# A slot table for each pass, scans in place of the decays, dt spread from SBUF, B turned once a chunk, and a second pass on 32 columns

## The chip, the cores and the metric

The kernel runs on one NeuronCore of one Trainium2 chip. The metric is the device time of one execution in microseconds (us), and the number quoted is the median over runs. Durations of instructions come from one profiled execution, which has a time of its own. The engines are called by their names in the profile: PE (matmul) and PEld (its weight load), DVE (vector), ACT (scalar), POOL and SP (which issues the DMAs).

## What is computed

The input x has shape (1, 64, 256, 128): 64 channels, T = 256 time steps, F = 128 frequencies, all in float32. Two layers follow each other.

Layer 0 runs Mamba blocks first along time and then along frequency, each in both directions. The core of one direction, with 128 inner channels and 16 states per channel, is

```
xz = in_proj(rmsnorm(u)); x, z = split(xz)
x  = silu(causal_conv4(x) + conv_b)
dt, B, C = split(x_proj(x), [4, 16, 16])
dt = softplus(dt_proj(dt) + dt_proj_b)
h[t] = exp(dt[t] * A) * h[t-1] + dt[t] * B[t] * x[t]      # per channel and state
y[t] = sum over states of h[t] * C[t]
out  = out_proj((y + x * Dp) * silu(z)) + u
```

The outputs of both directions go through one more linear map (tlin, flin) and are added to the input. Layer 1 normalises globally, runs a convolutional LSTM over 32 windows, and adds the result to its input. The change concerns layer 0 alone.

## The kernel before

**Tiling.** `Stage` is built twice: stage 0 is the pass along time, stage 1 the pass along frequency. A pass is cut into 64 chunks of 512 tokens (2 sequences of 256 steps, or 4 of 128). The inner channels lie on the 128 partitions. For the recurrence the 2048 pairs of channel and state in a direction are laid out again: the channels are cut into NB = 4 blocks of 32, and one block with 4 groups j of states fills 128 partitions. With two states g side by side this gives 8 **slots** a direction and 16 a chunk. One slot is one scan of 128 x 1024 elements.

**One slot S**, with its names and lines: `decays` (L599, ACT) makes dA = exp(A * dt) from rep, which holds dt repeated for the four state groups, into one of NRING = 4 buffers; a copy of zeros (L596) cuts the sequences apart. `inputs` (L579, PE) makes bx = dt * B * x in PSUM by 32 matmuls of dtxT (dt * x, turned) with D, a diagonal matrix that holds B; two buffers of two banks each. `recur` (L607, DVE) scans dA and bx into h, one of NH = 7 buffers. `outputs` (L613, POOL) multiplies h by C. `add_up` (L622, PE) folds the states of four slots into y in PSUM. In these matmuls the profile counts every float32 matmul as two passes.

**One chunk**: `load`, `squares`, `means` (pm), `rms`, `normalise` (unp, spread by DMA), `project_x` (px, L328 and L329), `project_z` (pz), `silus`, `step_sizes` (pv, L370), `softplus` (dt), `dt_away` (L394: dt goes to HBM four times, as the tile there), `spread_dt` (L486: rep comes back, 512 KB at a time), `project_bc` (pb, then bc, which holds B and C; C goes to HBM as away, L442), `spread_c` (L480), `times_x` (dtx, POOL), `turn` (dtx to pt and dtxT; B to bt, both by transposes on PE), and `diagonal` (L471, DVE: D = mask * bt, four times a direction). At the end of a direction `gate` multiplies y by silu(z) into yz (DVE, L638) and `skip` starts the next y as x * Dp (ACT). `close` (po) and `keep` finish the chunk.

**Order.** Every engine runs its instructions in the order in which they are emitted (a manual schedule). `run` walks through the slots; at slot S it emits the scan of S, the product of S - 1, the inputs and decays of S + 2, and then what the table HEAD names for that slot. HEAD is one list of (slot, step) for both passes; negative slots lie in the chunk before. All DMAs are issued from SP, in order too. `first` does the steps of a pass's first chunk by hand.

Of the kernel before, what the change touches and what calls it, by code (L numbers as in the profile page):

```python
# [29 lines left out]
F32 = mybir.dt.float32  # L30
# [30 lines left out]
NRING = 4  # L61
NREP = 3
RESPOND = 12
NH = 7
LAG = 2
# [7 lines left out]
HEAD = (  # L73
    (-12, "load"),
    (-7.5, "squares"),
    (-6, "means"),
    (-6, "rms"),
    (-5, "normalise"),
    (-2, "project_x", 0),
    (-1, "project_z"),  # L80
    (0, "project_x", 1),
    (6, "silus"),
    (6, "step_sizes"),
    (7, "softplus"),
    (8, "dt_away", 0),
    (8, "project_bc", 0, 1),
    (8.5, "times_x", 0),
    (9.5, "spread_dt", 0, 0),
    (10, "turn", 0),
    (10, "spread_c", 0, 0),  # L90
    (11, "diagonal", 0, 0, 0),
    (12, "spread_dt", 0, 1),
    (12.5, "times_x", 1),
    (13, "diagonal", 0, 0, 1),
    (13.5, "spread_c", 0, 1),
    (14, "dt_away", 1),
    (15, "diagonal", 0, 1, 0),
    (17, "diagonal", 0, 1, 1),
    (17, "spread_dt", 1, 0),
    (17.5, "spread_c", 1, 0),  # L100
    (18, "turn", 1),
    (19, "diagonal", 1, 0, 0),
    (20, "spread_dt", 1, 1),
    (21, "diagonal", 1, 0, 1),
    (21.5, "spread_c", 1, 1),
    (23, "diagonal", 1, 1, 0),
    (25, "diagonal", 1, 1, 1),
)
SECOND = tuple(x for x in HEAD if x[0] >= 12 and x[1] != "dt_away")


class Mamba:
# [3 lines left out]
    def __init__(self, ctx, tc, cols, room, d):  # L116
# [12 lines left out]
        for i in range(4):  # L129
            for n, t, rows, width in (  # L130
                ("g1", self.G1, P, P),
                ("g2", self.G2, P, P),
                ("wdt", self.Wdt, P, P),
                ("w2", self.W2, P, C),
            ):
                t.append(cp.tile([rows, width], F32, name=f"{n}{i}", tag=f"{n}{i}"))
        for i in range(2):
            self.Wz.append(cp.tile([P, P], F32, name=f"wz{i}", tag=f"wz{i}"))
            self.W3.append(cp.tile([P, 2, C], F32, name=f"w3{i}", tag=f"w3{i}"))
# [15 lines left out]
        self.xdt = take(RANK, 8, P).rearrange("p (i n) -> p i n", i=8)  # L155
# [13 lines left out]
    def load(self, first):  # L169
        dma, d = self.nc.sync.dma_start, self.d  # L170
        if first:
# [3 lines left out]
            dma(out=self.xdt, in_=d["dt_proj"])  # L175
# [22 lines left out]

    def dt(self, i, ps):
        self.nc.tensor.matmul(ps[:, 0:P], lhsT=self.xdt[:, i], rhs=self.xdt[:, 4 + i], start=True, stop=True)  # L200
        self.nc.vector.tensor_copy(self.Wdt[i], ps[:, 0:P])
# [23 lines left out]
class Stage:  # L225
# [8 lines left out]
    def __init__(self, ctx, m, stage, L, X, src, moments, gates):  # L234
# [5 lines left out]
        self.time = stage == 0  # L240
        n = f"s{stage}_"
        self.io = ctx.enter_context(tc.tile_pool(name=n + "io", bufs=1))
        self.wk = ctx.enter_context(tc.tile_pool(name=n + "wk", bufs=1))
        self.st = ctx.enter_context(tc.tile_pool(name=n + "st", bufs=NH))
# [5 lines left out]
        self.ps_bt = ctx.enter_context(tc.tile_pool(name=n + "bt", bufs=1, space=PSUM))  # L250
# [4 lines left out]
        self.zeros = fixed.tile([P, 2, 2, self.nseq // 2, 1], F32, name="zeros", tag="zeros")  # L255
        nc.gpsimd.memset(self.zeros, 0.0)
        self.dA = []
        for k in range(NRING):
            self.dA.append(fixed.tile([P, 2, 2, self.nseq // 2, L], F32, name=f"dA{k}", tag=f"dA{k}"))
        self.at, self.spare = {}, []  # L260

        self.y = self.ps_y.tile([P, NTOK], F32, name="y", tag="y")
# [29 lines left out]
    def means(self, ch):  # L292
        n = self.nseq // 2
        self.pm = self.mm("pm")[:, 0 : n * self.L].rearrange("p (n l) -> p n l", n=n)
# [8 lines left out]
    def normalise(self, ch):  # L303
        nc, n, L, unp = self.nc, self.nseq // 2, self.L, self.unp
        xn = self.io.tile([P, n, L], F32, name="xn", tag="xn")
        nc.gpsimd.tensor_mul(xn, self.at["u", ch], self.rs)
# [35 lines left out]
    def project_x(self, ch, d):  # L342
        i = 2 * self.stage + d
        px = self.mm("px")
        xs = self.wk.tile([P, NTOK], F32, name="xs", tag="xs", bufs=4)
# [4 lines left out]
    def project_z(self, ch):  # L350
        pz = [self.mm("pz") for _ in range(2)]
        self.gated(pz)
        for d in range(2):
            zs = self.wk.tile([P, NTOK], F32, name="zs", tag="zs", bufs=5)
# [11 lines left out]
    def step_size(self, ch, d):  # L366

        i = 2 * self.stage + d
        self.at["pv", d] = pv = self.mm("pv")
        self.nc.tensor.matmul(pv, lhsT=self.m.Wdt[i], rhs=self.at["xs", ch, d], start=True, stop=True)  # L370

    def step_sizes(self, ch):
        for d in range(2):
            self.step_size(ch, d)
# [8 lines left out]
    def softplus(self, ch):  # L383
        self.nc.scalar.preload_act_table_set(SOFTPLUS)
# [4 lines left out]
    def dt_away(self, ch, d):  # L389

        there = self.dram.tile([NJ, DB, NB, NTOK], F32, name="there", tag="there")
        for b in range(NB):
            dt = self.at["dt", ch, d][DB * b : DB * (b + 1)]
            self.nc.sync.dma_start(  # L394
                out=there[:, :, b].rearrange("j d t -> d j t"), in_=dt.unsqueeze(1).to_broadcast([DB, NJ, NTOK])
            )
        self.at["there", ch, d] = there

    def in_turns(self, ap, order):

        return ap.rearrange(order, i=2, u=NU)

    def times_x(self, ch, d):

        dtx = self.wk.tile([P, NTOK], F32, name="dtx", tag="dtx")
        natural, own = "p (i u c) -> p i u c", "p (u i c) -> p i u c"
# [7 lines left out]
    def project_bc(self, ch, *ds):  # L414
# [3 lines left out]
        for n in range(2):  # L418
# [13 lines left out]
            self.in_turns(bc[rows], "p (u i c) -> p i u c"), self.in_turns(pb[rows], "p (i u c) -> p i u c")  # L432
# [3 lines left out]
        for d in ds:  # L436
            away = self.dram.tile([NS // 2, NR, 2, 2, NTOK // 2], F32, name="away", tag="away")
            for g in range(2):
                first = 2 * NBC + NBC * d + NS // 2 * g
                c = bc[first : first + NS // 2].rearrange("p (i t) -> p i t", i=2)  # L440
                for i in range(2):
# [852 lines left out]
```

## Time and profile before

| | |
|---|---|
| median of 3 runs | 7161.71 us (7147.89 to 7171.97) |
| the profiled execution's own time | 7169.17 us |
| its span | 7167.4 us |
| first scan of pass one starts at | 45.46 us |
| last scan of pass one ends, first of pass two starts | 3211 us, 3243.5 us |
| last scan of pass two ends | 6473.5 us |
| the rest (LSTM) | 694 us |
| bytes moved by DMA | 921.86 MB, of which 310.38 MB written to HBM |

The profile's page lists the busy time of each engine and its share of the span, the groups of instructions with the idle time ahead of them and what ended it, and the DMA issues. A window gives the same busy times for a stretch; the two passes are two windows. The list of waits adds up, for each engine and line, the time for which it stood and whom it stood for. The timeline lists instructions in order of time. Overlap of one instruction's end with the next one's start makes the duration of an instruction some 80 ns longer than its share of a busy engine.

### The profile page before, as it was taken

The numbers are of one execution on the slowest core, as the hardware profiler recorded it, in microseconds if no ns is written. First come the engines' busy times: TensorE is split into PE (matmuls) and PEld (weight loads), VectorE is DVE, ScalarE is ACT, GpSimd is POOL, SyncE is SP. The second block draws the span as 40 slices with busy tenths as digits, with TensorE's granted clock in tenths as the row PEclk, the third lists the DMA queues.
The fourth block names the chain that finished last, engine by engine and source line by source line (L and its number), as shares of the span: only waits on it lengthen the run. The fifth ranks groups of instructions, "written<-read, shape, count | busy, mean of one in ns | idle before, by whom it ended". The sixth has DMA issues, their size and how long they took to land.

```text
span 7167.4 us, 327118 instructions
## 1 busy us (share of the span) xinstructions
PE 5830.0 (81%) x150024; PEld 3482.0 (49%) x150024; DVE 6368.4 (89%) x4166; ACT 4829.9 (67%) x8730; POOL 5567.1 (78%) x2898
## 2 busy tenths in 40 slices
PE   7878777777877787877888888787887878778998
PEld 4444444444444444444444444444444444447887
DVE  7999898889999999988988889999989899896887
ACT  6767676767767677767777677777767677763333
POOL 6888888778888888877887778888888788784554
PEclk9999999999999999999999899999999999999999
DMA  5555555555555555545555555555555555550000
GB/s 134 152 146 139 145 139 145 133 145 139 143 149 138 146 152 136 149 116 150 137 149 133 148 132 147 135 144 150 130 143 133 140 134 144 132 140 35 14 16 17
DMA packets 412666, 921.86 MB, mean 129 GB/s; under 512 B 52372, under 2 KB 142100, under 8 KB 411288
## 3 DMA queue, kind: packets, MB, share of 16 engines
q1 hardware_dynamic: 411288, 900.93, 48.8%
q8 instruction: 1177, 19.28, 1.1%
q14 instruction: 201, 1.65, 0.1%
HBM read 557.32 MB, written 310.38 MB: 121 GB/s over the span
## 4 chain that ended last, share of the span: by engine, by line
PE 25%; DVE 11%; ACT 8%; issue 6%; DMA 2%; POOL 2%; SPq 1%; DVEq 0%; POOLq 0%; ACTq 0%
DVE h L607 8%; PE bx L579 6%; PE cv L1048 6%; ACT dA L599 4%; PE y L622 3%; DVE D L471 2%; PE px L328 2%; PE px L329 1%; POOL h L613 1%; PE pv L370 1%; DMA unp<-xn 1%; PE pz L334 1%; PE pg L1104 1%; PE both L1160 1%; ACT L387 1%
## 5 line engine op out<-in xcount | busy, mean ns | idle before, releaser
L613 POOL TENSOR_TENSOR h<-h,C 128x1024 f32<-128x1024 f32 x2048 | 4826.7, 2374 | 974.8 <-DVE h L607 781.2
L607 DVE TENSOR_TENSOR_SCAN h<-dA,bx 128x1024 f32<-128x1024 f32 x2048 | 4618.0, 2276 | 497.4 <-PE bx L579 310.4
L579 PE MATMUL bx<-D,dtxT 64*32 64x128 f32 x131072 | 2509.0, 281 | 1180.5 <-DVE h L607 799.5
L579 PEld LDWEIGHTS bx<-D,dtxT 64*32 64x32 f32 x131072 | 1926.4, 108 | 2312.4 <-issue 1125.7
L599 ACT ACTIVATE dA<-rep,cols 128x510 f32<-128x510 f32 (+1 forms) x4096 | 2648.1, 710 | 171.2 <-DMA rep<-there 163.7
L471 DVE TENSOR_TENSOR D<-mask,bt 128x1024 f32<-128x1024 f32 x1026 | 1227.6, 1197 | 34.6 <-PE bt L458 34.0
L622 PE MATMUL y<-h,fold 128*32 128x512 f32 x8192 | 1106.4, 659 | 5.4 <-POOL h L613 5.4
L347 ACT ACTIVATE xs<-px,cols 128x512 f32<-128x512 f32 x252 | 173.4, 688 | 898.5 <-PE px L329 898.5
L622 PEld LDWEIGHTS y<-h,fold 128*32 128x32 f32 x8192 | 243.5, 117 | 612.8 <-issue 566.2
L407 POOL TENSOR_TENSOR dtx<-dt,xs 128x512 f32<-128x512 f32 x256 | 327.3, 1279 | 71.7 <-ACT dt L380 71.2
L460 ACT COPY dtxT<-pt 128x512 f32<-128x512 f32 x256 | 149.9, 585 | 300.6 <-PE pt L456 300.6
L328 PE MATMUL px<-unp,g 128*128 128x512 f32 x504 | 313.7, 706 | 46.5 <-DMA unp<-xn 46.3
L370 PE MATMUL pv<-xs,wdt 128*128 128x512 f32 x512 | 278.4, 669 | 34.0 <-ACT xs L364 31.8
L329 PE MATMUL px<-unp,g 128*128 128x512 f32 x504 | 277.3, 633 | 0.5 <-issue 0.5
L638 DVE TENSOR_TENSOR yz<-y,zs 128x512 f32<-128x512 f32 x256 | 172.7, 675 | 74.9 <-PE y L622 72.7
L355 ACT COPY zs<-pz 128x512 f32<-128x512 f32 x252 | 134.9, 586 | 154.5 <-PE pz L334 148.6
L1171 POOL TENSOR_TENSOR y<-v,X 128x512 f32<-128x512 f32 x32 | 40.6, 1269 | 231.2 <-DVE v L1169 231.2
L596 ACT COPY dA<-zeros 128x4 f32<-128x4 f32 (+1 forms) x1024 | 197.4, 193 | 5.4 <-DVE h L607 4.0
L634 ACT ACTIVATE y<-xs,cols 128x512 f32<-128x512 f32 x256 | 175.6, 686 | 9.5 <-DVE yz L638 9.5
L1120 ACT ACTIVATE a<-pg,cols,scale 128x488 f32<-128x488 f32 x128 | 86.5, 756 | 135.6 <-DVE pg L1118 135.6
L680 PE MATMUL po<-yz,w 128*64 128x256 f32 x1024 | 172.5, 400 | 0.9 <-ACT dA L599 0.9
L380 ACT ACTIVATE dt<-pv,cols 128x512 f32<-128x512 f32 x256 | 164.3, 684 | 12.7 <-issue 6.2
(190 smaller groups left out, 5195.8 us busy)
## 6 DMA issues: line engine op xcount, KB each, us to landing
there<-dt SPq DMA_DIRECT2D x1024, 256.0 KB
rep<-there SPq DMA_DIRECT2D x512, 512.0 KB
C<-away SPq DMA_DIRECT2D x512, 512.0 KB
away<-bc SPq DMA_DIRECT2D x1024, 32.0 KB
unp<-xn SPq DMA_DIRECT2D x504, 64.0 KB
u<-in_x SPq DMA_DIRECT2D x128, 64.0 KB
out<-y SPq DMA_DIRECT2D x32, 256.0 KB
w<-in_W_ih_f SPq DMA_DIRECT2D x10, 512.0 KB
```

The source lines that it names most:

```text
L328: nc.tensor.matmul(self.seqs(px), lhsT=m.G1[i], rhs=self.unp[:, :, first : first + L], start=True, stop=False)
L329: nc.tensor.matmul(self.seqs(px), lhsT=m.G2[i], rhs=self.unp[:, :, second : second + L], start=False, stop=True)
L370: self.nc.tensor.matmul(pv, lhsT=self.m.Wdt[i], rhs=self.at["xs", ch, d], start=True, stop=True)
L407: self.nc.gpsimd.tensor_mul(self.in_turns(dtx, own), self.in_turns(self.at["dt", ch, d], natural), self.in_turns(self.at["xs", ch, d], nat ...
L471: self.nc.vector.tensor_mul(D, self.m.mask.unsqueeze(1).unsqueeze(1).to_broadcast([P, n, 2, W]), b.unsqueeze(3).to_broadcast([P, n, 2, W]),)
L579: self.nc.tensor.matmul(bx[DB * j : DB * (j + 1), i, :, u], lhsT=dtxT[rows, u, DB * b : DB * (b + 1)], rhs=D[rows, u, j], start=True, stop ...
L596: nc.scalar.copy(dA[:, :, :, :, first : first + 1], self.zeros)
L599: nc.scalar.activation(dA[:, :, g, :, live], rep[:, :, :, live], AF.Exp, scale=m.A[:, k, n : n + 1])
L607: self.nc.vector.tensor_tensor_scan(h[:, step], dA[:, step], bx[:, step], 0.0, ALU.mult, ALU.add)
L613: self.nc.gpsimd.tensor_mul(h, h, self.at["C", ch, d, q])
L622: nc.tensor.matmul(y[DB * b : DB * (b + 1)].rearrange("p (i t) -> p i t", i=2), lhsT=self.m.fold, rhs=hs[b][:, g], start=False, stop=q == ...
L1048: self.nc.tensor.matmul(t[:, g, :, 0:n_out], lhsT=wts[s][:, gate * P : (gate + 1) * P], rhs=self.parts[n][:, :, s : s + n_out], start=s == ...
```

## The change

- **Tables.** HEAD becomes two tables, BY_Q for pass one and BY_HALF for pass two, with a slot for every piece of a chunk, four `spread_dt` a direction among them. `AT` gives the slots of fold, gate and close for each pass.
- **Scans write over decays.** dA and h are one tile: ACT writes the decays into h, the scan reads and overwrites it. There are 12 buffers in pass one, and 7 of double size in pass two. Decays are made four slots ahead. The zeros are written for every new tile.
- **dt from SBUF.** dt no longer goes to HBM: for each block b of 32 channels, four DMAs copy 32 rows of dt straight into the four quarters of rep.
- **dt projection.** The product of x_proj's dt rows and dt_proj is no longer formed (`dt` and `xdt` go). The dt rows ride with C in `project_bc`, and `step_size` multiplies 32 rows of bc by dt_proj, so it now follows `project_bc` and its copies.
- **B.** B of both directions is turned by four transposes of 64 rows into a fixed half bank (bt); pm, po and the LSTM's small sums use the other half of that bank (small).
- **Pass two 32-wide.** A slot there is two of the four sequences with four states, instead of four sequences with two. Chunks of 128 columns are cut into four rows of 32 instead of two of 64, so that D has 16 states by 32 columns, made in two products a direction instead of four. bx takes 32-row weights. C comes in one DMA of 1 MB a direction. The fold of a direction is done for the even slots and then for the odd ones, in 16 matmuls of 256 columns each.
- In the emitted order of pass two, the gate at slot 8k + 2 stands ahead of the odd slots' fold at the same slot: for that half of the tokens z multiplies what y holds by then, which is the skip term alone.

```diff
-NRING = 4
-NREP = 3
-RESPOND = 12
-NH = 7
-LAG = 2
+NSLOT = 12
+NPAIR = 7
+RESPOND = 13
+AHEAD = 2
+AT = ((2, 3, 3), (1, 2, 2))
-HEAD = (
...
-SECOND = tuple(x for x in HEAD if x[0] >= 12 and x[1] != "dt_away")
+BY_Q = (
+    (-11.5, "load"),
+    (-6.5, "squares"),
+    (-5.5, "means"),
+    (-5.5, "rms"),
+    (-4.5, "normalise"),
+    (-2, "project_x", 1),
+    (-1.5, "project_x", 0),
+    (0.5, "project_z"),
+    (7, "silus"),
+    (7, "project_bc", 0, 1),
+    (8, "softplus"),
+    (8.5, "c_away", 0),
+    (8.5, "c_away", 1),
+    (9, "times_x", 0),
+    (10, "spread_dt", 0, 0),
+    (10, "turn_b"),
+    (11.5, "spread_dt", 0, 1),
+    (11.5, "spread_dt", 0, 2),
+    (11.5, "turn_x", 0),
+    (12, "spread_dt", 0, 3),
+    (12.5, "diagonal", 0, 0, 0),
+    (13.5, "diagonal", 0, 0, 1),
+    (14, "diagonal", 0, 1, 0),
+    (15.5, "spread_dt", 1, 0),
+    (15.5, "diagonal", 0, 1, 1),
...
+    (19, "diagonal", 1, 0, 0),
+    (21, "diagonal", 1, 0, 1),
+    (21, "spread_c", 1, 0),
+    (24, "diagonal", 1, 1, 0),
+    (24, "spread_c", 1, 1),
+    (25, "diagonal", 1, 1, 1),
+)
+BY_HALF = (
...
+    (-7, "means"),
+    (-7, "rms"),
+    (-5.5, "normalise"),
+    (-1.5, "project_x", 0),
+    (1, "project_z"),
+    (4, "project_x", 1),
+    (6, "silus"),
+    (6, "project_bc", 0, 1),
+    (7.5, "softplus"),
+    (7.5, "spread_dt", 0, 0),
+    (7.5, "turn_b"),
+    (8, "c_away", 0),
+    (8.5, "times_x", 0),
+    (9, "diagonal", 0, 0, 0),
...
+    (11, "diagonal", 0, 0, 1),
...
+    (14, "diagonal", 1, 0, 0),
...
+    (18, "diagonal", 1, 0, 1),
+    (19, "spread_dt", 1, 2),
+    (22.5, "spread_c", 1, 0),
+)
...
     def step_size(self, ch, d):
...
-        self.nc.tensor.matmul(pv, lhsT=self.m.Wdt[i], rhs=self.at["xs", ch, d], start=True, stop=True)
+        rows = slice(2 * NBC + NBC * d, 2 * NBC + NBC * (d + 1))
+        self.nc.tensor.matmul(pv, lhsT=self.m.Wdt[self.stage][rows], rhs=self.bc[rows], start=True, stop=True)
...
+    def turn_b(self, ch, ds=(0, 1)):
+        nc = self.nc
+        rows = slice(NBC * ds[0], NBC * (ds[-1] + 1))
+        for u in range(NU):
+            nc.tensor.transpose(
+                self.bt[:, ds[0] : ds[-1] + 1, u], self.bc[rows, P * u : P * (u + 1)], self.m.ident[rows, rows]
+            )
...
-        t = self.wk.tile([P, 2, NTOK], F32, name="rep", tag="rep", bufs=NREP)
-        there = self.at["there", ch, d].rearrange("j d b t -> (j d) b t")
-        self.nc.sync.dma_start(out=t, in_=there[:, 2 * h : 2 * h + 2])
+        t = self.wk.tile([P, NTOK], F32, name="rep", tag="rep", bufs=6 if self.time else 3)
+        for j in range(NJ):
+            self.nc.sync.dma_start(
+                out=t[DB * j : DB * (j + 1)], in_=self.at["dt", ch, d][DB * b : DB * (b + 1)]
+            )
...
+    def decays(self, k):
+        nc, m, L = self.nc, self.m, self.L
+        ch, d, _, b = self.where(2 * k)
+        first, live = self.ends(d)
+        h = self.st.tile([P, 4, 4, L], F32, name="h", tag="h")
+        nc.scalar.copy(h.rearrange("p i s t -> p (i s) t")[:, :, first], self.zeros)
+        rep = self.at["rep", ch, d, b].rearrange("p (i l) -> p i l", i=4)
+        for s in range(4):
+            n = 4 * b + s
+            nc.scalar.activation(h[:, :, s, live], rep[:, :, live], AF.Exp, scale=m.A[:, 2 + d, n : n + 1])
...
     def recur(self, S):
...
-        h = self.st.tile([P, 2 * NTOK], F32, name="h", tag="h")
-        dA = self.dA[S % NRING].rearrange("p i g n l -> p (i g n l)")
-        bx = self.at.pop(("bx", S)).rearrange("p i g u c -> p (i g u c)")
-        self.nc.vector.tensor_tensor_scan(h[:, step], dA[:, step], bx[:, step], 0.0, ALU.mult, ALU.add)
+        h = self.at["h", S][:, step]
+        bx = self.at.pop(("bx", S)).rearrange("p i s u c -> p (i s u c)")[:, step]
+        self.nc.vector.tensor_tensor_scan(h, h, bx, 0.0, ALU.mult, ALU.add)
...
+    def sums(self, S):
+        n = S - self.fold_at
+        if self.time:
+            return range(n - 4, n) if n > 0 and n % 4 == 0 else ()
+        first = n // 8 * 8 - 8 + n % 8
+        return range(first, first + 8, 2) if n % 8 < 2 and n >= 8 else ()
+
+    def ahead(self, S):
+        if self.time:
+            for n in (4, 5) if S % 16 == self.pause else () if S % 16 == self.pause + 1 else (4,):
+                if 0 <= S + n < 16 * NCH:
+                    self.decay(S + n)
+        elif S % 2 == 0 and 0 <= S + 4 < 16 * NCH:
+            self.decays(S // 2 + 2)
```

## The prediction

> **What bounds the kernel now.** I read the page's busy line first, then the two Mamba passes as windows, then DVE's waits, then the groups, then the timeline.
>
> ```profile
> PE 5830.0 (81%) x150024; PEld 3482.0 (49%) x150024; DVE 6368.4 (89%) x4166; ACT 4829.9 (67%) x8730; POOL 5567.1 (78%) x2898
> ```
> ```profile
> 45.00:3211.00 3166.00, 2518.90 (x73223) 1415.77 (x73216) 2910.42 (x1660) 2258.34 (x4007) 2605.61 (x1212) 0.96 0.55 142
> 3243.00:6473.00 3230.00, 2605.98 (x73385) 1472.70 (x73378) 2910.11 (x1660) 2294.35 (x4217) 2607.91 (x1212) 0.93 0.55 139
> ```
> The columns of the windows are length, then busy time of PE, PEld, DVE, ACT, POOL, clock, DMA share, GB/s. Each window is 64 chunks of 16 slots. Per chunk, pass one takes 3166/64 = 49.5 us and pass two 50.5; DVE is busy 45.5 in both, PE 39.4 and 40.7, POOL 40.7, ACT 35.3 and 35.8. VectorE bounds both passes, with 256 and 320 us of idle time left, and PE and POOL stand only 5 us a chunk behind it.
>
> ```profile
> L613 POOL TENSOR_TENSOR h<-h,C 128x1024 f32<-128x1024 f32 x2048 | 4826.7, 2374 | 974.8 <-DVE h L607 781.2
> L607 DVE TENSOR_TENSOR_SCAN h<-dA,bx 128x1024 f32<-128x1024 f32 x2048 | 4618.0, 2276 | 497.4 <-PE bx L579 310.4
> ...
> L599 ACT ACTIVATE dA<-rep,cols 128x510 f32<-128x510 f32 (+1 forms) x4096 | 2648.1, 710 | 171.2 <-DMA rep<-there 163.7
> L471 DVE TENSOR_TENSOR D<-mask,bt 128x1024 f32<-128x1024 f32 x1026 | 1227.6, 1197 | 34.6 <-PE bt L458 34.0
> ```
> ```profile
> DVE h L607 <- PE bx L579: 310.4, 261, 4.5
> DVE h L607 <- ACT dA L599: 157.8, 96, 10.1
> DVE yz L638 <- PE y L622: 72.7, 66, 6.0
> ```
> A chunk is 16 scans, 8 products D and 2 products with z. DVE's idle time is mostly scans waiting for bx, then for decays. The timeline of DVE (columns: start, duration) gives the pitch, start to start, which is what an instruction really costs here:
>
> ```profile
> 3258.10 1.20 DVE L471 TENSOR_TENSOR D<-mask,bt 128x1024 f32<-128x1024 f32 x1
> 3259.21 4.46 DVE L607 TENSOR_TENSOR_SCAN h<-dA,bx 128x1024 f32<-128x1024 f32 x2
> ...
> 3265.18 4.46 DVE L607 TENSOR_TENSOR_SCAN h<-dA,bx 128x1024 f32<-128x1024 f32 x2
> 3269.55 1.20 DVE L471 TENSOR_TENSOR D<-mask,bt 128x1024 f32<-128x1024 f32 x1
> ```
> D takes 3259.21 - 3258.10 = 1.11 us, a scan (3269.55 - 3265.18)/2 = 2.19.
>
> [...] 2276 ns against 1197 for a product of the same size, so writing over the decays saves no scan time. [...]
>
> **The change, part by part.**
>
> *Second pass 32-wide.* D holds 16 states by 32 columns instead of twice 8 by 64: two products a direction instead of four. 64 chunks x 4 x 1.11 = 284 us off the bounding engine, 41.0 us a chunk left (45.5 - 4.4). bx keeps 32 matmuls of 128 columns a slot, now on 32 rows; as in each u eight different tiles are addressed, I take today's 1.16 us. Bounds: half of that if row tiles overlap further (no gain, it is not the bound), or twice, the second rival. The fold becomes 16 matmuls of 256 columns instead of 8 of 512: a wave of four took 0.43 us (1.86 a fold); po's 256-column waves took 0.24, so 8 x 0.24 = 1.9: +0.1 to +0.2 us a fold, beside the scans.
>
> *Slots and order in pass one.* What DVE loses now comes in slots 15, 1 and 3, where px (1.9 us), pz (1.1), px and a fold (1.86) stand between two bx; these prices are start to start in the timeline between 1500 and 1550 us, as are po and the waves below and above. PE has two bx buffers, so PE work between two bx is free only up to 2 x 2.19 - 2 x 1.2 = 2.0 us, plus 1.11 for each D on DVE meanwhile. The table puts both px (3.8 us) at slot 14, and D at 12, 13, 14 and 15. Worked from scan 14's end: bx of 16 at 0 to 1.2, px to 5.0, bx of 17 to 6.2; DVE runs D to 1.1, scan 15 to 3.3, D to 4.4, scan 16 to 6.6: no wait. pz follows bx of 18 and a fold bx of 19, each with one slot of room; pb waits for the silus at slot 7, under D at 8 and 9. With decays four slots ahead in place of two, the 158 us of waits for ACT go too. What is late next is chance, such as this stop of PE in the middle of a tile, which DVE's next scan waits out:
>
> ```profile
> 1540.87 1.12 PE L579 MATMUL bx<-D,dtxT 64*32 64x128 f32 x60
> ...
> 1544.94 0.41 PE L579 MATMUL bx<-D,dtxT 64*32 64x128 f32 x4 [2.95 <-issue]
> ...
> 1545.49 2.29 DVE L607 TENSOR_TENSOR_SCAN h<-dA,bx 128x1024 f32<-128x1024 f32 x1 [1.87 <-PE bx L579]
> ```
> PE's waits put 372 us in 266 times to "issue" before bx. I keep 1.1 us a chunk: 45.5 + 1.1 = 46.6, so 2982 us, **-184**. Bounds: -256 (no idle) and 0.
>
> *Order in pass two.* Three engines then want about 41 us, and the order shows two waits. (a) px of direction 1 is at slot 4, the silus and pb at slot 6. Let T be scan 4's end: bx of 6 to T+1.2, px to 3.1, its copy 0.7, a pair's decays 2.7, table load 1.3, two silus 1.2: T+9.0; pb 0.9, then bx of 9, queued behind it, 1.2: T+11.1. Scans 5 to 8 end at T+8.8: DVE waits 2.3 us. (b) At slots 2 and 10 the odd slots' fold writes y after the gate has read it, so PE waits for the gate; at slot 2 bx of 4, po (1.5 us) and bx of 5 stand behind it, 1.9 + 1.2 + 1.5 + 1.2 = 5.8 us against two scans, D and the room of one buffer, 1.11 + 2 x 2.19 - 0.4 = 5.1: 0.7 us. The skip on ACT waits for that fold too, and the next decays behind it are four slots early. With 1.2 of chance: 41.0 + 2.3 + 0.7 + 1.2 = 45.2, 2893 us, **-337**. Bounds: 42 (waits hidden) and 48.
>
> *dt from SBUF.* Out go 8 there and 4 rep issues a chunk (268 MB of the 310 written to HBM); in come 32 rep issues of 32 partitions. SP's tile views give the prices:
>
> ```profile
> L394 SPq DMA_DIRECT2D there<-dt x1024: 302/456/1977, 17.2 to 6420.8; - x171
> L486 SPq DMA_DIRECT2D rep<-there x512: 325/346/1510, 21.4 to 6441.5; - x171
> ```
> At 0.35 to 0.6 us (unp's median is 605 ns) they cost SP 11 to 19 us, with 8.5 for C, away, unp and u: under 28 of 46. Twelve of them and four away stand ahead of unp's four, which px waits for. Counted from scan 5's end, where pass one's fold at slot 6 is next on PE: the fold ends at 3.1, ACT's decays, table load and silus at 7, pb at 7.9, the bc copies at 9.3; away (4 x 0.66) is issued by 12, dt ready at 11.9, rep by 17 to 19, xn ready on POOL at 18, unp issued by 20.4. Today unp's last issue ends at 1534.4 and px still waits for it until 1539, so 4.5 us more, 25; px's turn on PE comes at 26. Free, with 1 us of room, and each us beyond it would cost DVE up to one a chunk, 64 a pass.
>
> *B's bank.* bt, pm, po and made share one bank, so PE's pm waits for D at slot 9, and D at slot 11 for ACT's read of pm. I place that read 0.7 us before D: free; bounds 0 and +1 us a chunk, 64 us. Two pv on 32 rows each save PE up to 0.9 us, and 4 transposes 0.4: no cost, no gain for DVE. pv now waits for bc's copies; ACT waits 1 us with two slots of decays in hand.
>
> *The rest.* Zeros are written in every slot of pass one: 8 x 0.19 = 1.5 us of ACT a chunk, beside scans (ACT 36.8 of 46.6); uncovered it would be 97 us. POOL's product reads C in runs of 128 or 256; the strided dtx (128x512, 1279 ns) costs what the contiguous y does (1269), so 2374 stays. It waits for dt before the next dtx, and may lag by some slots, since seven pairs of h hold 14; 10% more would make POOL 45 us a chunk and the equal of DVE in pass two. The start (first scan at 45 us) and the gap between passes (32 us) lose the trip through HBM: **-10** together, bounds -25 and +10.
>
> Sum: 7169.2 (the profiled execution's own time, span 7167.4) - 184 - 337 - 10 = 6638. It lies 7.5 above the median, so 6630.
>
> **Rivals.** *The idle time stays* (20%): the new waits give back what the order wins, and only the 284 us of D go: 7169 - 284 - 7 = 6878. For it: PE and POOL lie so close behind. Against: the lead of four slots. *All of it goes* (6%): 6878 less most of the 576 us of idle time, about 6380; POOL's 41 us a chunk leaves no more. *SP becomes the bound, slower* (6%): some there issues took up to 1.98 us. Place: rep, 32 a chunk. With r a rep issue, a chunk takes 32r + 8.5; it decides from r = 1.2, and at 1.3 both passes take 50.1: 128 x 50.1 against 6396 now, 7180 to 7210. Against: the median of a plain 128-row rep is 0.346. *32-row tiles don't overlap* (4%): bx at twice its time adds 16 x 0.9 = 14 us to PE's 40.7, pass two 55 a chunk, 7270.
>
> **How the numbers follow.** The working above has 62%, between 6460 and 6800; 2% is left for a cancellation. Faster 0.88, same 0.02, slower 0.10; a measurement of this kernel tells about 0.3%, 21 us, from no change. The range reaches from 6440 to 6920, over the idle-stays case.
>
> **What would show it.** Right: D some 768 times, scans still near 2276 ns, DVE idle 1 us a chunk in pass one and 4 in pass two, there mostly before slot 9's scan, PE waiting for ACT's silus before pb; HBM writes near 42 MB. Wrong: rep's issue over 1 us, bx of pass two over 1.2 us a slot, POOL's product above 2.5 us, or DVE waiting for ACT before D or before scans.

## The result, and the profile after

The changed kernel takes 7131.57 us, the kernel before 7159.40 on the same chip: a ratio of 0.9971, 95% interval 0.9953 to 0.9988. It is 28 us faster, where 530 were forecast. The profiled execution took 7122.5 us, 484 more than the sum of 6638.

The busy line and the row of TensorE's granted clock on the page of the kernel after (40 slices, in tenths):

```profile
PE 6045.9 (85%) x153608; PEld 3714.3 (52%) x153608; DVE 6092.0 (86%) x3904; ACT 4860.7 (68%) x9242; POOL 5532.1 (78%) x2898
...
PEclk9999999999999999977777887887888787879999
```

DVE lost its 276 us (6368.4 to 6092.0), as planned; but PE, which has hardly more to do, is busy 216 us longer, and from the 18th slice, where pass two begins, to its end the clock stands at 0.7 to 0.8. The two passes as windows, columns as in the prediction:

```profile
45.00:3086.00 3041.00, 2478.07 (x72960) 1382.23 (x72960) 2896.96 (x1660) 2284.73 (x4514) 2590.90 (x1213) 0.94 0.45 105
3125.00:6425.00 3300.00, 2855.82 (x77178) 1734.87 (x77170) 2650.01 (x1405) 2293.47 (x4212) 2586.16 (x1213) 0.80 0.42 96
```

Pass one fell from 3166 to 3041 us (47.5 a chunk). Pass two rose from 3230 to 3300 (51.6 a chunk), with DVE idle for 650 us and PE, at a clock of 0.80 instead of 0.93, busy for 2856. The excess over the forecast is 59 us in pass one (against 2982), 407 in pass two (against 2893) and 18 between the passes (a gap of 40 us and an unmoved start, against 10 us saved): 484 in all.

The groups of the page after that answer to those of before:

```profile
L686 POOL TENSOR_TENSOR h<-h,C 128x1024 f32<-128x1024 f32 x2048 | 4794.8, 2373 | 662.0 <-DMA C<-away 460.9
L679 DVE TENSOR_TENSOR_SCAN h<-h,bx 128x1024 f32<-128x1024 f32 x2048 | 4588.4, 2274 | 634.7 <-PE bx L637 621.1
...
L466 PE MATMUL pb<-xs,wbc 128*32 128x512 f32 x1024 | 260.8, 855 | 214.1 <-ACT xs L421 212.5
```

Scan and product kept their durations; the scans' idle time grew from 497 to 635 us, and nearly all of it is for bx. Of this pass two holds most, in the list of DVE's waits for its window:

```profile
DVE h L679 <- PE bx L637: 525.5, 390, 6.9
```

PE's timeline in a chunk of pass two shows two causes side by side:

```profile
4515.61 1.13 PE L385 MATMUL px<-unp,g 128*128 128x512 f32 x2
...
4519.24 1.15 PE L637 MATMUL bx<-D,dtxT 32*32 32x128 f32 x64 [0.56 <-DVE h L679]
4522.92 2.45 PE L466 MATMUL pb<-xs,wbc 128*32 128x512 f32 x8 [2.53 <-ACT xs L421]
...
4543.06 1.96 PE L637 MATMUL bx<-D,dtxT 32*32 32x128 f32 x64 [0.31 <-DVE h L679]
...
4545.86 1.91 PE L385 MATMUL px<-unp,g 128*128 128x512 f32 x2
```

The first is the wait for the silus ahead of pb. The second is that the same 64 passes of bx (32 matmuls of the program) take 1.15 us at one place and 1.96 at another, and that two passes of px, 1.13 us earlier in the same chunk, take 1.91. The trace's record of the clock stands at half from 4539.7 to 4549.9 us, and in this stretch tiles of 128 rows take longer like the 32-row ones: px, and pt with 1.11 us at 4544.95 against 0.66 at 4536.95. This record has two values alone, 1.0 and 0.5. Half holds for 1310 of the 3300 us of pass two here, and for 447 of its 3230 us in the kernel before.

### The profile page after: what moved, and what is told of

Its sections match the earlier page's. It is cut to its first block, busy times and chain, and to the rows that moved or that the text cites. A ratio compares the mean times of both kernels' runs of the same rounds, so it can differ in the third digit from the quotient of the medians.

```text
span 7120.8 us, 337921 instructions
## 1 busy us (share of the span) xinstructions
PE 6045.9 (85%) x153608; PEld 3714.3 (52%) x153608; DVE 6092.0 (86%) x3904; ACT 4860.7 (68%) x9242; POOL 5532.1 (78%) x2898
## 3 DMA queue, kind: packets, MB, share of 16 engines
q8 instruction: 1204, 19.73, 1.2%
HBM read 289.00 MB, written 41.94 MB: 46 GB/s over the span
## 4 chain that ended last, share of the span: by engine, by line
PE 40%; DVE 7%; ACT 5%; issue 3%; POOL 1%; DMA 0%; SPq 0%; ACTq 0%; DVEq 0%; POOLq 0%
PE bx L637 12%; PE y L697 7%; PE cv L1136 6%; DVE h L679 6%; ACT h L671 2%; PE px L385 2%; PE pb L466 2%; PE px L386 2%; PE pv L427 1%; ACT L417 1%; PE pz L391 1%; PE pt L508 1%; PE aux L772 1%; PE pg L1192 1%; PE both L1248 1%
## 5 line engine op out<-in xcount | busy, mean ns | idle before, releaser
L686 POOL TENSOR_TENSOR h<-h,C 128x1024 f32<-128x1024 f32 x2048 | 4794.8, 2373 | 662.0 <-DMA C<-away 460.9
L679 DVE TENSOR_TENSOR_SCAN h<-h,bx 128x1024 f32<-128x1024 f32 x2048 | 4588.4, 2274 | 634.7 <-PE bx L637 621.1
L637 PE MATMUL bx<-D,dtxT 64*32 64x128 f32 (+1 forms) x131072 | 2572.4, 293 | 647.2 <-DVE h L679 508.2
L637 PEld LDWEIGHTS bx<-D,dtxT 64*32 64x32 f32 (+1 forms) x131072 | 2014.3, 112 | 1702.2 <-DVE h L679 887.0
L659 ACT ACTIVATE h<-rep,cols 128x510 f32<-128x510 f32 x2048 | 1356.1, 715 | 60.8 <-DMA rep<-dt 56.5
L671 ACT ACTIVATE h<-rep,cols 128x508 f32<-128x508 f32 x2048 | 1303.3, 708 | 2.8 <-DMA rep<-dt 2.2
L697 PE MATMUL y<-h,fold 128*32 128x256 f32 (+1 forms) x12288 | 1189.4, 519 | 68.8 <-issue 56.6
L521 DVE TENSOR_TENSOR D<-mask,aux 128x1024 f32<-128x1024 f32 x512 | 613.5, 1199 | 27.9 <-ACT X L778 22.6
L466 PE MATMUL pb<-xs,wbc 128*32 128x512 f32 x1024 | 260.8, 855 | 214.1 <-ACT xs L421 212.5
L521 DVE TENSOR_TENSOR D<-fold,aux 128x1024 f32<-128x1024 f32 x256 | 309.0, 1208 | 67.3 <-ACT made L918 29.3
L385 PE MATMUL px<-unp,g 128*128 128x512 f32 x504 | 326.1, 734 | 20.5 <-DMA unp<-rs 17.2
L508 PE MATMUL pt<-ident,dtx 128*128 128x128 f32 x1024 | 202.4, 330 | 54.1 <-POOL dtx L452 53.9
```

The lines of the kernel that those rows point to most:

```text
L385: nc.tensor.matmul(self.seqs(px), lhsT=m.G1[i], rhs=self.unp[:, :, first : first + L], start=True, stop=False)
L466: nc.tensor.matmul(pb[first : first + NBC], lhsT=self.m.Wbc[:, 2 * self.stage + d, n], rhs=self.at["xs", ch, d], start=True, stop=True,)
L521: self.nc.vector.tensor_mul(self.at["D", ch, d, q][:, own], mask.unsqueeze(1).unsqueeze(1).to_broadcast(shape), self.bt[:, d, own, n * q : ...
L637: self.nc.tensor.matmul(bx[DB * j : DB * (j + 1), i, :, u], lhsT=dtxT[rows, u, DB * b : DB * (b + 1)], rhs=D[rows, u, n_j * j : n_j * (j + ...
L659: nc.scalar.activation(h[:, :, g, live], rep[:, :, live], AF.Exp, scale=m.A[:, d, n : n + 1])
L671: nc.scalar.activation(h[:, :, s, live], rep[:, :, live], AF.Exp, scale=m.A[:, 2 + d, n : n + 1])
```

## Experiments: the clock

The theory put first is that the 32-row tiles of bx lower the granted clock; the rivals are the waits of the new order.

**rows64: the kernel after, with bx of pass two on 64 rows.** Each product then adds the tokens of two blocks of 32 where one belongs, so the values of pass two differ.

```diff
-                    rows = slice(K * (first + i), K * (first + i + 1))
+                    rows = slice(K * (first + i), K * (first + i + 1)) if self.time else slice(W * i, W * (i + 1))
```

> The kernel after, with bx of pass two on 64 rows instead of 32 (the same 32 matmuls a slot, the same columns and order; it adds up rows of a second block, so B's product in pass two is another one). Theory 1, the clock: [...] (0.80 in pass two against 0.94 in pass one). Then the clock of pass two returns to about 0.93, DVE's stalls at slots 1 and 9 shrink by half, pass two goes from 3300 to about 3050 us and the time to about 6880. Theory 2, the order: the waits of PE for the silus and for the gate cost the time and the clock alike. Then nothing moves: 7130 within 20 us, clock of pass two 0.80. Theory 3, PE is simply full in pass two (2856 of 3300 us busy): nothing moves either.

**before_rows32: the kernel before, with bx of pass two on 32 rows** (the other half of the rows is left out).

```diff
-                    rows = slice(W * i, W * (i + 1))
+                    rows = slice(W * i, W * (i + 1)) if self.time else slice(W * i, W * i + DB)
```

> The kernel before, with bx of pass two on 32 rows instead of 64 (it leaves out half of the rows of each product). Order, counts and columns stay. Theory 1 (32-row tiles lower the clock): the clock of pass two falls from 0.93 to about 0.80 and the kernel gets slower, 7260 to 7460 us. Theory 2 (the order does it) and theory 3 (PE is full): 7160 within 20 us, clock unchanged.

**wide: pass two in the form of pass one** (64-row tiles, table BY_Q, four products D a direction, folds of 512 columns, 12 buffers of h).

```diff
-AT = ((2, 3, 3), (1, 2, 2))
+AT = ((2, 3, 3), (2, 3, 3))
...
-        self.rows, self.nq = (2, 2) if self.time else (4, 1)
-        self.order = BY_Q if self.time else BY_HALF
+        self.rows, self.nq = 2, 2
+        self.order = BY_Q
...
```

> The kernel after, with pass two in the form and order of pass one (64-row bx, four products D a direction, folds of 512 columns, the table of pass one, gate after the fold). Theories 1 and 2 alike: pass two takes the 47.5 us a chunk of pass one, 3040 us instead of 3300, so about 6870, although DVE has 284 us more of D to do; clock about 0.94. If something of pass two itself is slow (C, the LSTM's small sums, the residual from X), it stays above 49 us a chunk, 6970 or more.

| kernel | median us | ratio to before, 95% | pass two us | clock in pass two |
|---|---|---|---|---|
| after | 7131.57 | 0.9971 (0.9953 to 0.9988) | 3300 | 0.80 |
| rows64 | 6964.75 | 0.9717 (0.9697 to 0.9738) | 3104 | 0.92 |
| before_rows32 | 7368.31 | 1.0286 (1.0243 to 1.0328) | 3451 | 0.80 |
| wide | 6937.07 | 0.9683 (0.9659 to 0.9707) | 3078 | 0.94 |

Pass two of rows64, of before_rows32 and of wide, as windows:

```profile
3172.00:6276.00 3104.00, 2540.45 (x77170) 1567.50 (x77170) 2628.47 (x1404) 2290.51 (x4212) 2588.03 (x1212) 0.92 0.45 102
```
```profile
3264.00:6715.00 3451.00, 2979.76 (x73378) 1648.87 (x73378) 2920.84 (x1660) 2299.79 (x4216) 2605.33 (x1212) 0.80 0.51 130
```
```profile
3152.00:6230.00 3078.00, 2518.33 (x73120) 1418.76 (x73120) 2898.37 (x1660) 2325.41 (x4724) 2593.02 (x1212) 0.94 0.44 103
```

The number of PE's instructions is the same with and without the edit (77170 and 77178, 73378 and 73385); only the rows of a tile differ. Added to the kernel before, 32 rows bring the clock from 0.93 to 0.80 and 204 us (7368.31 - 7163.84); taken out of the kernel after, they bring it back to 0.92 and take 167 us off. That is less than the 250 expected; DVE's stall at slot 9 fell only from 3.6 to 3.1 us a chunk. So in these runs the tile's rows lower the clock, with either order of work, and the order alone does not (0.93 in the kernel before, 0.92 in rows64).

How long PE is busy does not say when the clock is halved. In the traces of the kernels before and after, the recorded clock changes only on a grid of 3.41 us. Of the windows of that length in pass two that ran at full clock with PE busy for 50 to 70% of the time, 4 of 103 were followed by half clock in the kernel before, 54 of 65 in the kernel after and 83 of 99 in before_rows32. At full clock a 32-row tile takes as long as a 64-row tile (1.15 and 1.16 us for 64 passes). What in the 32-row tiles brings the half clock is not shown: bx ran on 32 and on 64 rows alone.

wide does without the 32-wide form, pays back the whole 284 us of D, and is still no slower than rows64 (it stayed 67 us above the 6870 expected). What the 32-wide form saves on DVE is thus not collected even at the better clock. Why, is the second question.

## Experiments: the order of pass two

With the clock back, pass two of rows64 takes 3104/64 = 48.5 us a chunk, against 45.2 forecast. The runs stand on several chips, so they are compared by their ratio to the kernel before on the same chip. The table gives DVE's idle time by slot in pass two, us a chunk, the mean over 64 chunks, worked out from the trace ("slots 3 to 5" is all between the ends of scans 2 and 5, with the gate and D there; "10 to 12" likewise between scans 9 and 12). The last two columns part the chunks by whether PE stops in them: stands for over 2 us with nothing to wait for that the profile shows. They give the length of such a chunk, from its first scan to that of the next, and in brackets how many of the first 63 there are.

| kernel | slots 3 to 5 | slot 9 | slots 10 to 12 | ratio, 95% | with a stop, us | without, us |
|---|---|---|---|---|---|---|
| rows64 | 3.3 | 3.1 | 0.4 | 0.9717 (0.9697 to 0.9738) | 50.3 (35) | 46.4 (28) |
| rows64_ready | 3.8 | 0 | 3.8 | 0.9788 (0.9749 to 0.9827) | 51.5 (41) | 46.8 (22) |
| rows64_gate5 | 2.6 | 3.5 | 0.7 | 0.9776 (0.9738 to 0.9814) | 50.7 (33) | 47.8 (30) |
| rows64_ready_gate5 | 1.7 | 0 | 4.9 | 0.9778 (0.9746 to 0.9811) | 52.6 (21) | 47.9 (42) |
| rows64_defer | 3.5 | 0 | 4.4 | 0.9773 (0.9736 to 0.9809) | 50.8 (41) | 47.3 (22) |
| rows64_defer_gate5 | 3.2 | 0 | 3.7 | 0.9725 (0.9672 to 0.9777) | 50.8 (42) | 46.4 (21) |
| rows64_act4 | 3.2 | 4.5 | 0.6 | 0.9860 (0.9814 to 0.9905) | 51.7 (39) | 47.7 (24) |
| rows64_act12 | 3.5 | 3.1 | 0.4 | 0.9734 (0.9700 to 0.9769) | 50.5 (36) | 46.7 (27) |
| wide | 0.4 | 0 | 0 | 0.9683 (0.9659 to 0.9707) | 50.0 (10) | 47.9 (53) |

The stops are the first part of the answer. In rows64 31 of its 37 lie in slot 2, and a chunk with one is 3.8 us longer, with DVE idle for 5.6 us in slots 0 to 5 instead of 1.4; slot 9's stall is the same with and without (3.0 and 3.2). On the mean over all chunks this is 2.1 us. Where no stop falls, the 32-wide form is 1.4 us a chunk ahead of wide; but wide has 10 stops, rows64 37. What the traces show of the stops stands in the last section. That it lengthens the chunk is read from the chunks side by side; no run took the stops away.

**pb_later, gate_later, order2, order2_rows64: moves in the table.** They begin from the kernel after. pb_later puts `project_bc` at slot 7 instead of 6. gate_later changes AT of pass two to (1, 3, 3). order2 does both and moves softplus, turn_b, away and D of direction 0 by one slot or more; order2_rows64 adds the 64 rows.

```diff
-    (6, "project_bc", 0, 1),
+    (7, "project_bc", 0, 1),
```

> The kernel after, with pb of pass two at slot 7 instead of 6, so that bx of slot 9 no longer queues behind a matmul that waits for ACT's silus. Theory 2 (order): DVE's stall before slot 9's scan (3.7 us a chunk) goes for the most part, 2.5 to 3.5 us x 64 = 160 to 220, so 6910 to 6970[...]. Theory 1 (clock): the stall before slot 9 goes too, as bx is ahead of pb, but px at half clock keeps its 1.7 us at slot 1 and the clock stays near 0.80; about 7000, as later steps (pv, turn_b) slip by a slot. Theory 3: less than 50 us gained, the stall comes back in the next slots.

> The kernel after, with the gate, skip and close of pass two at slot 8k+3 instead of 8k+2, so after the odd slots' fold: PE no longer waits for the gate before that fold. With bx on 64 rows DVE still lost 3 us a chunk between slots 3 and 5, so if that wait is the cause, 2 to 3 us x 64 = 130 to 190 go and the time is 6940 to 7000. If PE at a lower clock is the cause of the late bx there, under 60 us go: 7070 or more.

> The same, and in pass two also pb at slot 7, pv and B's turn at 8.5, D at 10.5 and 12 instead of 9 and 11: every matmul that needs ACT is emitted a slot after what ACT needs for it. If the two waits cost what the stalls of the 64-row run say (3.1 us before slot 9's scan, 3 about slot 4), pass two falls from 51.5 to about 45 to 46 us a chunk: 6720 to 6790. The clock stays at about 0.80, since bx is still on 32 rows. Rival: PE at that clock is full, the stalls come back in other slots, and 7000 or more is left.

> The last one with bx of pass two on 64 rows (it adds up rows of a second block, so B's product is another one): both causes taken away. 42.5 to 44 us a chunk, 6570 to 6670, clock 0.93. If it is no faster than the order alone, the clock costs nothing once the order has slack.

pb_later: 7136.0 us, 0.9959 (0.9938 to 0.9979), like after, where 6910 to 7000 were expected of either cause alone. The stall ahead of slot 9 went, and D waits for the turned B in its place, in the list of DVE's waits of pb_later:

```profile
DVE D L521 <- PE aux L498: 208.1, 63, 4.0
```

gate_later: 7227.41, 1.0076 (1.0047 to 1.0104). zs has four buffers, and the next chunk's copy of pz at slot 1 now waits for the gate at slot 3 (156 us on ACT in 62 waits), so the silus are late, and slot 9's wait is 4.9 us. With this order the gate reads y after both folds, so that all four sequences keep their sums over the states, where the kernel after leaves those of two out; order2, the runs with gate5 and those with wide keep them too. order2: 7349.66, 1.0240 (1.0206 to 1.0274); order2_rows64: 7236.40, 1.0096 (1.0073 to 1.0119). Here D stands in its queue until ACT has read pm from B's bank (407 us of DVE's waits in order2), and the decays between silus and softplus cost one more table load (1.28 us at L671 in the trace of order2_rows64). Three moves, three new waits: 6720 to 6790 were expected of order2 and 6570 to 6670 of order2_rows64, and both are slower than the kernel before. Between these two the rows of bx are worth 113 us again, at mean clocks of 0.854 and 0.920 over the whole execution.

**rows64_ready, rows64_gate5, rows64_ready_gate5: the two waits taken away.** ready lets pb of pass two read a tile that has long been there, so that B, C and dt are made of other data; gate5 is the later gate with five buffers of zs.

```diff
-                    rhs=self.at["xs", ch, d],
+                    rhs=self.at["xs", ch, d] if self.time or not ch else self.unp[:, :, 3 : 3 + self.L],
...
-AT = ((2, 3, 3), (1, 2, 2))
+AT = ((2, 3, 3), (1, 3, 3))
...
-            zs = self.wk.tile([P, NTOK], F32, name="zs", tag="zs", bufs=5 if self.time else 4)
+            zs = self.wk.tile([P, NTOK], F32, name="zs", tag="zs", bufs=5)
...
```

> The kernel after with bx of pass two on 64 rows, and pb of pass two reading an input that has long been ready instead of the silus of xs; B, C and dt of the second pass are then made of other data, with the same instructions. It asks whether wait (a) of the prediction is what stands before slot 9. Theory A (PE's wait for the silus makes bx of 9 late): the stall before slot 9's scan falls from 3.1 us a chunk to under 0.8, no other grows, pass two goes from 48.5 to about 46 us a chunk, 64 x 2.4 = 150 us: near 6810. Theory B (ACT's queue sets the pace: the copies of pb stand behind the silus there, and pv, dt and D follow them): slot 9's stall goes, but D of slots 9 to 11 or the scans after it wait instead; 6910 to 6965.

> The kernel after with bx of pass two on 64 rows, the gate of pass two one slot later (AT of pass two 1, 3, 3) and five buffers of zs there in place of four. It asks whether wait (b) of the prediction, the odd fold at slots 2 and 10 that waits for the gate, is what stands before slots 3 to 5. Here the skip, and so the next odd fold, follow a slot later, with bx of 4 and 5 ahead of them. Theory A (order of PE at the gate): the 3.0 us a chunk of stalls in slots 3 to 5 falls to about 1, with no ACT wait of zs for the gate: 64 x 2 = 130 us, near 6835. Theory B (ACT waits for the fold before the decays and hands the delay on, wherever the gate stands): the decays, px and the silus come later still, slot 9's stall grows by what slots 3 to 5 win: 6940 to 7020.

> Both edits together: pb of pass two reads a ready input (B, C and dt of that pass are made of other data), the gate of pass two is at slot 3 with five zs buffers, bx on 64 rows. If the two waits are separate, as the prediction counts them, their gains add up: 45.0 us a chunk in pass two or less, near 6700, and VectorE is left with 4 us a chunk. If one chain through ACT joins them, the pair gives no more than the better of the two alone, within 30 us.

6987.62, 6983.06 and 6983.02 us: none gains on rows64, neither by the ratio nor in the chunks without a stop. DVE's waits in pass two, of rows64 and then of rows64_ready:

```profile
DVE h L679 <- PE bx L637: 416.9, 271, 6.9
```
```profile
DVE h L679 <- PE bx L637: 274.1, 334, 7.8
DVE D L521 <- PE aux L498: 126.3, 63, 2.6
```

The wait for bx of slot 9 is gone, and the time comes back at D (2.0 us a chunk), at the gate and at the scans after it: the bc copies still stand behind four silus on ACT, and pv and the transposes of B behind them. Theory B, one chain through ACT, fits all three (only rows64_ready lies above the range given for it, 6910 to 6965). The chain can be read in ACT's timeline of rows64:

```profile
4521.09 0.22 ACT L667 COPY h<-zeros 128x16 f32<-128x16 f32 x1 [3.31 <-PE y L697]
4521.26 2.55 ACT L671 ACTIVATE h<-rep,cols 128x508 f32<-128x508 f32 x4
...
4524.87 2.55 ACT L671 ACTIVATE h<-rep,cols 128x508 f32<-128x508 f32 x4
4528.17 0.69 ACT L404 ACTIVATE xs<-px,cols 128x512 f32<-128x512 f32 x1 [0.75 <-PE px L386]
...
4528.85 2.55 ACT L671 ACTIVATE h<-rep,cols 128x508 f32<-128x508 f32 x4
4531.41 1.28 ACT L417 ACT_TABLE_LOAD   x1
4532.70 1.15 ACT L421 ACTIVATE xs<-xs 128x512 f32<-128x512 f32 x2
```

It begins with a wait of ACT for the odd slots' fold at slot 2: only then are two of the seven double buffers of h free for the decays. The 3.31 us are a long one, as a stop of 2.27 us falls into this fold; the mean over the chunks is 1.4. From there to the table load after the softplus, which ends at 4540, ACT waits once, for 0.75 us, with three pairs of decays ahead of the silus. DVE meanwhile needs 2.19 us a slot and catches up with it.

**rows64_defer, rows64_defer_gate5: ACT's order.** The pair of decays of slot 6 is made after the softplus.

```diff
-        elif S % 2 == 0 and 0 <= S + 4 < 16 * NCH:
-            self.decays(S // 2 + 2)
+        elif S % 2 == 0:
+            for n in () if S % 16 == self.pause else (2, 4) if S % 16 == self.pause + 2 else (4,):
+                if 0 <= S + n < 16 * NCH:
+                    self.decays((S + n) // 2)
```

> bx of pass two on 64 rows, and ACT does the pair of decays of slot 6 after the softplus, with the pair of slot 8, instead of ahead of the silus; all else as in rows64, and every value is computed as before. Theory B (ACT's order is the one chain): the silus come 2.8 us earlier, and pb, bc, pv, dt, bt and D with them; slot 9's stall falls from 3.1 us a chunk to under 0.8 and D at slot 10 does not wait in its place; 6964 - 64 x 2.3 = near 6815. Rival (the two pairs after the softplus are late themselves): scans 10 or 11 wait for ACT's decays by 2 us or more a chunk, 6930 to 7000. Rival (PE's stops and folds in slots 2 to 5 set the pace, and ACT has no part): the silus are no earlier, 6965.

> The same with the gate of pass two at slot 3 and five buffers of zs. With ACT's order loosened, a later gate can show its gain: the stalls of slots 3 to 5 (3.5 us a chunk in rows64) fall by 1 to 2 us, 60 to 130 us under rows64_defer. If these stalls are PE's own (px, the fold and po in four slots, with the stops in the middle of a tile), it is within 25 us of rows64_defer.

6982.20 and 6965.74 us. The first rival came true: the stall moves from slot 9 to scan 10, which now waits for the deferred decays. With the later gate as well, 60 to 130 us more were expected to go; the 16 that went are within the 25 given for stalls of slots 3 to 5 that are PE's own (px, the fold, po and the stops). DVE's waits in pass two of rows64_defer:

```profile
DVE h L679 <- PE bx L637: 292.3, 222, 6.9
DVE h L679 <- ACT h L671: 179.1, 54, 3.6
```

A stall that keeps its size (3.1, then 3.3 us) when the work is moved suggests a stretch in which ACT has too much work, not a wrong order of it. Two runs tried that.

**rows64_act4, rows64_act12: 1.4 us more of ACT.** Two of a pair's four decays are written twice, with the same values, at slot 4 or at slot 12.

```diff
-        for s in range(4):
+        for s in (0, 0, 1, 1, 2, 3) if k % 8 == 4 else range(4):
```

> rows64, with two of the four decays of the pair done at slot 4 of pass two written twice: 2 x 0.71 = 1.4 us more of ACT a chunk, the same values, nothing else moved. Theory B (ACT sets the pace from slot 3 to slot 10): paid in full, 64 x 1.3 = +80 us, 7030 to 7060, the stall at slot 9 grows from 3.1 to about 4.4 us. Rival (PE and its stops set it, ACT has slack): within 25 us of rows64, 6965 to 6990.

> The same two decays written twice, but of the pair done at slot 12, where ACT waits 5 us a chunk for px, rep and pz before slot 2. Theory B: absorbed there, 0 to +25 us, 6965 to 6990. If ACT's total of work sets the pace wherever it lies: +80 us as in the first.

At slot 4 slot 9's stall grew from 3.1 to 4.5 us, and pass two from 3104 to 3204 us: paid in full. At slot 12 the stall stayed at 3.1, and pass two took 3124, within what one execution differs from the next here (pass one, untouched by any of these edits, took 3037 to 3088). The chunks say the same: with 1.4 us more of ACT at slot 4 those without a stop grow by 1.3 us and those with one by 1.5, at slot 12 by 0.2 both. So ACT sets the pace between slot 4 and slot 9, and not at slot 12; a stop in slot 2 delays its start and adds to it.

**wide_early_d, wide_mm: on the best form.** wide_early_d takes D of slot 21 to slot 19; wide_mm puts pm and po into the ring of two banks, so that B's bank is shared with the gates alone.

```diff
-        self.pm = self.small.rearrange("p (n l) -> p n l", n=n)
+        self.pm = self.mm("pm")[:, 0 : NTOK // 2].rearrange("p (n l) -> p n l", n=n)
...
-        self.po = self.small
+        self.po = self.mm("po")[:, 0 : NTOK // 2]
```

> The kernel with pass two in pass one's form, with D of slot 21 at slot 19, ahead of po and of ACT's read of po, which lie in B's bank. DVE waits 45 and 30 us there for ACT's read of po in the two passes. If the shared bank causes that, about 60 to 75 us go, 6870; rival: po now waits for two D on DVE and bx behind it comes late, 6940 or more.

> Pass two in the form and order of pass one (64-row tiles, four products D a direction), with pm and po of both passes in the ring of two banks that px, pz, pb, pv and pt use, so that B stands alone in its bank but for the gates. Theory A (the shared bank costs what the traces put to D behind ACT's read of po, 30 to 45 us a pass): these waits go and nothing takes their place: 6937 - 70 = about 6865. Theory B (the ring of two is full: px and pz wait for ACT's reads of pm and po): PE waits at px, pz or pb grow and DVE's waits for bx with them: 6935 to 7020.

wide_early_d: 6993.41, 0.9753 (0.9732 to 0.9774), slower than wide, as its rival had it: with D earlier, scans wait 349 us for bx, 230 in wide. wide_mm: 6911.51, 0.9671 (0.9629 to 0.9713). D's waits for ACT's read of po (45 and 30 us in wide's passes) are gone, but the interval does not part it from wide. wide and wide_mm are the fastest versions seen, some 230 us below the kernel before.

## Why the prediction was wrong, step by step

- **Right.** D runs 512 + 256 = 768 times, DVE's busy time in pass two is 2650/64 = 41.4 us a chunk (41.0 said), scan (now writing over the decays) and product keep 2274 and 2373 ns, HBM writes are 41.94 MB. A rep issue has a median of 589 ns, inside 0.35 to 0.6: SP did not become the bound.
- **The step that failed** is "I take today's 1.16 us" for 32-row bx. The tile itself holds that price at full clock (1.15 us); what was left out is that its rows lower the clock, under which px, pb, pt and the folds run too (844, 1017, 361 and 441 ns a pass between 3172 and 6200 us of the kernel after, 660, 838, 316 and 405 in rows64; px by L385). The bounds given (half, or twice with 14 us a chunk) were the author's estimates of how tiles overlap, the wrong question; the trace of the kernel before shows 64 passes of bx in 1.16 us, where one takes 281 ns, and no 32-row tile. Size: 3300 - 3104 = 196 of the 484 us. In chunks without a stop it is more, 50.9 against 46.4 us; in rows64 PE also stops more often (37 times against 17), and that takes some back.
- **Chance, the second term at fault.** The prediction saw a stop of PE, called such stops chance, and kept 1.2 us a chunk for them in pass two and 1.1 in pass one. In pass two of rows64 they cost 2.1 on the mean. In pass one of the kernel after DVE is idle for 2.3 us a chunk: 1.6 in the 45 chunks without a stop and 4.0 in the 18 with one.
- **Waits (a) and (b)** were found but counted as two small separate sums. As sizes they were near: without stops a chunk of rows64 is 41.1 us of DVE's work, 3.2 of wait at slot 9 (2.3 said), 1.4 in slots 0 to 5 (0.7 said for (b)) and 0.7 elsewhere. From scan 4's end to scan 9's start pass 12.3 us on the mean, 11.1 said. What failed in "41.0 + 2.3 + 0.7 + 1.2" is that the terms are not separate: the waits lie on one chain, fold to ACT to silus to B to D, whose own length sets the pace, so removing either frees nothing. With the stops this makes the other 3104 - 2893 = 211 us.
- **Pass one**: 47.5 us a chunk against 46.6, 59 us in all. DVE's waits there are 96 us for bx, 23 at D for ACT's read of po and 16 at the gate. Chunks without a stop take 46.8, so the order did nearly what was worked out for it.
- **B's bank, free**: this held in effect. D does wait there, by 23 us in pass one, but wide_mm shows no measurable gain from removing it.
- **Start and gap**: -10 was expected, the gap grew from 32 to 40 us. This was not tried apart.
- **The rivals.** The two slower ones lie nearest in size (7180 to 7210 and 7270), but by luck: neither is what happened, as a rep issue has a median of 589 ns and 32-row bx keeps 1.15 us at full clock. "The idle time stays" (6878) is nearest to what is seen once the clock is back: 6965, with DVE idle for 665 us in the two passes of rows64, 576 before.

## What to carry to other kernels

Ask of a smaller matmul tile not only what it costs but what it does to the clock of everything else on PE: compare the clock of the stage before and after (0.93 and 0.80 here). When waits are priced one by one, look for the engine that joins them; double a suspected piece of work inside the stretch and outside it, and see which one is paid. Here a stall that moved with its size unchanged was a sign of too much work in a stretch, and moving instructions within it gained nothing. Before a stop is called chance, see whether it always falls at the same place of the program, and compare the chunks with it to those without.

## What the runs showed of the hardware that was not expected

A stage whose matmuls mostly use tiles of 32 rows ran at a mean clock of 0.80, with tiles of 64 rows at 0.92 and 0.93 at the same number of instructions (pass two of after and before_rows32, of rows64 and before). And PE stops in the middle of a tile with nothing to wait for that the profile shows, as here in rows64's fold:

```profile
4516.60 0.63 PE L697 MATMUL y<-h,fold 128*32 128x256 f32 x4
4519.50 1.92 PE L697 MATMUL y<-h,fold 128*32 128x256 f32 x28 [2.27 <-issue]
```

The page of the kernel after lists an instruction queue of 1204 packets (19.73 MB); with the 2 x 153608 instructions of PE and its weight loads, that is one packet to 255 of them. In pass two of rows64 PE stopped so for over 2 us 37 times, 122 us in all. Counted in blocks of 256 from PE's first instruction in the trace, each of the 37 stops stands ahead of instruction 192 or 193 of its block. Each ends 1.2 to 1.7 us after the end of a packet of that queue; only 12% of the pass lies 1.2 to 1.8 us behind one. In the two passes of all 18 kernels the place holds for 911 of 915 such stops and the packet for all of them (1.2 to 1.8 us). The stop that the prediction shows, 2.95 us long, stands at such a place too. Packets come every 5.1 us on the mean in pass two of rows64, but the one ahead of a stop's end comes 9 us after the one before. What makes a stop, and whether the packets have a part in it, is not shown: no run tried to move one.
